# Context attentions of small heads: values of two periods and pieces of two periods in turn between the two blocks of a period

## The chip, the cores and the metric

The kernel runs on one core of a Trainium2 chip. The metric is the device time of one execution in microseconds (us); lower is better. Before the change three runs gave 2829.77 us as their median, from 2824.37 to 2834.39. The engines are called by the profile's names: PE (matmuls), PEld (loads of a matmul's stationary operand, which overlap PE), DVE (vector), ACT (activation), POOL and SP (which issues the transfers).

## The reference, cut to what matters

The reference is a decoder of four layers on 4 sequences of 256 tokens of width 128, in fp32. Two of its twelve blocks concern us: the cross attentions of layers 0 and 2, which attend to a context of 1601 rows of width 96 with 16 heads of 8.

```
q = (x @ Wq).reshape(B, N, 16, 8);  k, v likewise from the context (1601 rows)
scores = einsum('bhid,bhjd->bhij', q, k) * 8 ** -0.5      # layer 0 also masks
attn = softmax(scores, axis=-1)
out = einsum('bhij,bhjd->bhid', attn, v).reshape(B, N, 128)
```

Layer 0 multiplies the result by Wo, layer 2 sends it through a small feed forward net; each then adds the residual and normalises. The rest (band attention, two mixtures of experts, self attentions, linear attention, a wide cross attention, a quantised layer) is the same in both kernels.

## The kernel before, in words

The kernel is one program of eight stages. The stages `l0_xattn` (L1105) and `l2_xattn` (L1545) both call `context_heads` (L832), which the change rewrites in part. It works on 16 groups, each a batch element and four heads; a head sits in a strip of 32 partitions, so the matmuls of four heads can run on the PE at once, each in a strip of 32 rows of the array.

A group takes 7 periods, numbered p over the whole stage. The softmax needs the largest score of each query before it can take exponentials, so each group is worked through twice:

- `maxima` (L881) computes scores with the queries on the output's partitions, 458 keys at a time, and reduces them on DVE (L898) to a maximum. After the seventh part one more reduction (L904) writes the maxima to a padded tile.
- `shift` (L954) transposes the maxima on the PE and subtracts them (L535, DVE) from the queries.
- `scores` (L907), 9 periods after the maxima of the same group, computes shifted scores the other way round, for 256 keys, as two accumulations of 128 keys; ACT takes the exponential (L921) into tiles `E`.
- `sums` (L924), 10 periods after, multiplies the values with `E` and accumulates in one PSUM bank, `acc`, of which there is one (`bufs=1`, L928). In the `sums` matmuls all 128 rows of the array work, in strips of 32 columns. After the seventh period of a group ACT copies `acc` away (L939).

In one period the maxima are computed for heads 0 and 1, then for heads 2 and 3; the scores for heads 2 and 3 first and then for 0 and 1. So a half of `maxima` and a half of `scores`, written one after the other, fill the array's four row strips. Such a pair of halves is called a block here: two maxima tiles and two score tiles. A period has two blocks; the first is called A and the second B.

The other pieces are called from a table `other`, by period: `queries`, `keys` (four parts), `values` (four parts) and `shift`. With them go the steps of generators in `later`, one step a period (`advance`, L366): the end of a group (transposes, division), the output projection, the residual, the norm, and behind them other blocks of the network (`l0_ffn` and the queries of layer 1 in one stage, the end of `block1` with `l2_attn`, L1471, and `l2_gate`, L1587, in the other). Some of these steps use POOL, and one issues the transfer of the weights `p3_0` on SP.

PE, DVE and ACT take their instructions in the order in which the program writes them (`manual_schedule`). PSUM holds 7 banks that are given out in turn by `misc` (L349) and the one bank of `acc`. A block takes four of the seven, a piece one or two. So a tile's bank is that of the seventh tile before it, and its first matmul waits until that one has been read. `E` tiles turn over in the same way.

Of the kernel before, what the change touches and what calls it, by code (L numbers as in the profile page):

```python
# [21 lines left out]
B, T, D = 4, 256, 128  # L22
P = 128
# [6 lines left out]
NE, FM = 8, 408  # L30
# [272 lines left out]
class Net:  # L303
# [528 lines left out]
    def context_heads(self, query, wk, wv, done):  # L832
# [6 lines left out]
        nc = self.nc  # L839
        groups = [(b, kt, r) for b in range(B) for kt in range(2) for r in range(2)]  # L840
        n_groups, n_pairs = len(groups), len(groups) // 2
        scale = 8**-0.5
        vs = []
        for i in range(3):
            t = self.tile(f"V{i}", [P, NCH, 4, SW], bufs=1)
# [61 lines left out]
        def scores(i, k, jp):  # L907
            cs = range(2 * k, min(2 * k + 2, NCH))
            kp = min(P, S2 - 2 * k * P)
            w = len(cs) * T  # L910
            heads = [(j, self.misc()) for j in range(2 * jp, 2 * jp + 2)]
            for c in cs:
                for j, ps in heads:
                    r = slice(SW * j, SW * j + KR)
                    o = (c - 2 * k) * T
                    self.mm(
                        ps[:kp, o : o + T], ks[i // 2][r, c * P : c * P + kp], q2s[i][r, :]
                    )
            for j, ps in heads:
                e = self.tile("E", [P, 512], bufs=8)  # L920
                nc.scalar.activation(e[:kp, :w], ps[:kp, :w], AF.Exp, scale=scale)  # L921
                es[i, k, j] = e

# [34 lines left out]
        for t in range(n_pairs):  # L958
            for at, what in (
                (-4, (queries, t)), (-3, (keys, t, 0)), (-2, (keys, t, 1)), (-1, (keys, t, 2)),  # L960
                (1, (keys, t, 3)), (7, (shift, 2 * t)), (14, (shift, 2 * t + 1)),
            ):
                other.setdefault(14 * t + at, []).append(what)
        for b in range(B):
# [2 lines left out]

        engines = {nc.tensor.engine, nc.vector.engine, nc.scalar.engine}
        with self.tc.manual_schedule(engines=engines):
            for p in range(-4, 7 * n_groups + 10):  # L970
                (m, s, v) = (
                    divmod(p - lag, 7) if 0 <= p - lag < 7 * n_groups else None
                    for lag in (0, 9, 10)
                )
                if m:
                    maxima(*m, 0)
                if s:
                    scores(*s, 1)
                if v:
                    sums(*v)  # L980
                if m:
                    maxima(*m, 1)
                if s:
                    scores(*s, 0)
                for f, *args in other.pop(p, ()):
                    f(*args)
                self.advance(later)
            while later:
                self.advance(later)

# [480 lines left out]
    def l2_attn(self, b):  # L1471
        nc = self.nc
        x, xT = self.x[b], self.xT[b]
        ps = self.misc()
        for n in range(NB):
            self.mm(ps[:, n * D : (n + 1) * D], xT[:, n * P : (n + 1) * P], self.w("p2", "Wq"))
        pq = ps[:, : NB * D].rearrange("p (n d) -> p n d", n=NB)
        neg = self.tile("neg", [P, NB])
        nc.vector.tensor_reduce(neg, pq, AX.X, ALU.max, negate=True)
        q = self.tile("q", [P, NB, D], bufs=1)  # L1480
        sums = self.tile("sums", [P, NB])
        for n in range(NB):
            nc.scalar.activation(
                q[:, n, :], pq[:, n, :], AF.Exp, bias=neg[:, n : n + 1],
                accum_out=sums[:, n : n + 1],
            )
        ps = self.misc()
        self.mm(ps[:, :T], self.w("p2", "Wk"), xT)
        neg = self.tile("neg2", [P, 1])
        nc.vector.tensor_reduce(neg, ps[:, :T], AX.X, ALU.max, negate=True)  # L1490
        kT = self.tile("kT", [P, T], bufs=1)
        rk = self.tile("rec2", [P, 1])
        nc.scalar.activation(kT, ps[:, :T], AF.Exp, bias=neg, accum_out=rk)
        yield
        nc.vector.reciprocal(rk, rk)
        rec = self.tile("recs", [P, NB])
        nc.vector.reciprocal(rec, sums)
        for n in range(NB):
            nc.vector.tensor_scalar(
                q[:, n, :], q[:, n, :], rec[:, n : n + 1], D**-0.5, ALU.mult, ALU.mult  # L1500
            )
        ps = self.misc()
        for n in range(NB):
            nc.tensor.transpose(
                ps[:, n * P : (n + 1) * P], kT[:, n * P : (n + 1) * P], self.ident
            )
        for n in range(NB):
            self.mm(
                ps[:, T + n * D : T + (n + 1) * D], xT[:, n * P : (n + 1) * P],
                self.w("p2", "Wv"),  # L1510
            )
        kv = self.tile("kv", [P, 2, NB, D], bufs=1)
        nc.scalar.copy(kv.rearrange("p k n d -> p (k n d)"), ps)
        yield
        qT = self.transposed(q, "qT", engine=nc.scalar)
        yield
        ps = self.misc()
        for n in range(NB):
            self.mm(ps[:, :D], kv[:, 0, n, :], kv[:, 1, n, :], start=n == 0, stop=n == NB - 1)
        cx = self.tile("cx", [P, D], bufs=1)  # L1520
        nc.vector.tensor_scalar_mul(cx, ps[:, :D], rk)
        yield
        yield
        ps = self.misc()
        self.mm(ps[:, :T], cx, qT)
        aT = self.tile("aT", [P, T], bufs=1)
        nc.scalar.copy(aT, ps[:, :T])
        yield
        yield
        ps = self.misc()  # L1530
        for n in range(NB):
            to = ps[:, n * D : (n + 1) * D]
            self.mm(to, aT[:, n * P : (n + 1) * P], self.w("p2", "Wo"), stop=False)
            self.bias_mm(to, self.w("p2", "bo", 1))
        y = self.residual(b, ps[:, : NB * D])
        z = yield from self.normed_steps(y, "xn")
        wide = [P, NB, D]
        nc.gpsimd.tensor_mul(z, z, self.w("p2", "gamma").unsqueeze(1).broadcast_to(wide))
        nc.gpsimd.tensor_add(z, z, self.w("p2", "beta").unsqueeze(1).broadcast_to(wide))
        yield  # L1540
        y = self.y()
        nc.vector.tensor_add(y, z, x)
        yield from self.block_end_steps(b, y)
# [43 lines left out]
    def l2_gate(self, b):  # L1587

        nc = self.nc
        wide = [P, NB, NE]  # L1590
        ps = self.misc()
        for n in range(NB):
            to = ps[:, n * NE : (n + 1) * NE]
            self.mm(to, self.xT[b][:, n * P : (n + 1) * P], self.w("p2", "gw"), stop=False)
            self.bias_mm(to, self.w("p2", "gb", 1))
        pl = ps[:, : NB * NE].rearrange("p (n e) -> p n e", n=NB)
        neg = self.tile("neg", [P, NB])
        nc.vector.tensor_reduce(neg, pl, AX.X, ALU.max, negate=True)
        s = self.tile("gate", wide)
        sums = self.tile("sums", [P, NB])  # L1600
        for n in range(NB):
            nc.scalar.activation(
                s[:, n, :], pl[:, n, :], AF.Exp, bias=neg[:, n : n + 1],
                accum_out=sums[:, n : n + 1],
            )
        yield
        rec = self.tile("recs", [P, NB])
        nc.vector.reciprocal(rec, sums)
        nc.vector.tensor_mul(s, s, rec.unsqueeze(2).broadcast_to(wide))
        v1, one1 = self.top(s)  # L1610
        yield
        v2, one2 = self.top(self.without(s, one1))
        yield
        tot = self.tile("p", [P, NB])
        nc.vector.scalar_tensor_tensor(tot, v1, 1e-20, v2, ALU.add, ALU.add)
        nc.vector.reciprocal(tot, tot)
        nc.vector.tensor_mul(v1, v1, tot)
        nc.vector.tensor_mul(v2, v2, tot)
        nc.vector.tensor_mul(one1, one1, v1.unsqueeze(2).broadcast_to(wide))
        nc.vector.tensor_mul(one2, one2, v2.unsqueeze(2).broadcast_to(wide))  # L1620
        gate = self.tile("gates", wide, bufs=4, pool=self.act)
        nc.vector.tensor_add(gate, one1, one2)
        yield
        ps = self.misc()
        for n in range(NB):
            nc.tensor.transpose(ps[:NE, n * P : (n + 1) * P], gate[:, n, :], self.ident)
        wT = self.tile("wT", [NE, T])
        nc.scalar.copy(wT, ps[:NE, :T])
        yield
        ps = self.misc()  # L1630
        for n in range(NB):
            self.mm(
                ps[:, n * D : (n + 1) * D], wT[:, n * P : (n + 1) * P], self.w("p2", "db", NE)
            )
        return gate, self.residual(b, ps[:, : NB * D])
# [496 lines left out]
```

## Time and profile before

| what | value |
|---|---|
| median of 3 runs | 2829.77 us (2824.37 to 2834.39) |
| the profiled execution: its own time, its span | 2829.03 us, 2827.2 us |
| PE, DVE, ACT busy in the span | 95%, 64%, 54% |
| `l0_xattn`: first maxima to last `sums` matmul | 49.7 to 544.7 us |
| `l2_xattn`: the same | 841.9 to 1344.5 us |
| window 73 to 515 us (full periods of the first): PE, DVE, ACT busy | 433.75, 283.13, 246.41 of 442 us |
| window 875 to 1316 us (full periods of the second) | 432.86, 285.51, 237.48 of 441 us |

An instruction's line gives what it writes and reads (`one` is a tile from `misc`). `one<-K,Q` are the maxima, `one<-Q,K` the scores, `acc<-E,V` the sums, `one<-ctx,w` the keys, `one<-xT,w` the queries. An fp32 matmul shows as two passes, each with its own weight load, so `x16` of `acc<-E,V` is eight matmuls of the program. Matmuls in different strips overlap, and PE counts as busy as long as one of them is running.

### The profile page before, as it was taken

Reading aid. Unit: us, or ns where it says so; the run is one execution under the profiler, and the core shown is the slowest. Engines: PE = TensorE matmul, PEld = TensorE weight load, DVE = VectorE, ACT = ScalarE, POOL = GpSimd, SP = SyncE. Lnnn points to the kernel's source line nnn. Section 1 sums busy time; section 2 is a strip of 40 time slices with the busy share of each in tenths; the row PEclk is TensorE's granted clock in tenths of the full one; section 3 lists DMA queues with packets and bytes.
Section 4 is the critical chain, followed back from the end, with each engine's and each line's share of the span. In section 5 each row is a group of like instructions: output and inputs, shape, how many; then the busy total and the mean of one; then the engine's idle time right before and its main releaser. Section 6 shows DMA issues by size and latency. Waiting matters only on the chain.

```text
span 2827.2 us, 62963 instructions
## 1 busy us (share of the span) xinstructions
PE 2696.4 (95%) x27003; PEld 1776.1 (63%) x27003; DVE 1803.9 (64%) x3946; ACT 1533.0 (54%) x2943; POOL 178.4 (6%) x191
## 2 busy tenths in 40 slices
PE   7999999898889999999999999998999999999997
PEld 4555565566655555555897777776656666666664
DVE  6656666364567665664455766665757777777775
ACT  2555555455534555555553444445656666666564
POOL 2000110110010000000001111101100000000000
PEclk9999999999989999999999999999999999999999
DMA  3000000000020000000002000000000000000000
GB/s 114 1 2 1 2 1 2 1 1 1 1 79 23 1 2 1 1 2 1 1 1 103 2 14 2 2 2 2 2 1 2 3 2 2 3 1 2 3 1 3
DMA packets 5223, 27.65 MB, mean 10 GB/s; under 512 B 584, under 2 KB 2764, under 8 KB 3408
## 3 DMA queue, kind: packets, MB, share of 16 engines
q1 hardware_dynamic: 4944, 23.62, 2.4%
q8 instruction: 212, 3.47, 0.5%
q14 instruction: 67, 0.55, 0.1%
HBM read 23.07 MB, written 0.52 MB: 8 GB/s over the span
## 4 chain that ended last, share of the span: by engine, by line
PE 87%; DVE 8%; ACT 2%; issue 1%; DMA 0%; POOL 0%; POOLq 0%; ACTq 0%; DVEq 0%; SPq 0%
PE one L388 63%; PE big L388 13%; PE acc L388 8%; DVE M L898 1%; PE one L533 1%; PE one L824 1%; PE one L461 1%; DVE St L1974 1%; DVE mpad L686 1%; DVE Ms L681 1%; ACT w L1313 0%; ACT E L720 0%; PE one L1323 0%; DVE w L1940 0%; DVE ln_st L475 0%
## 5 line engine op out<-in xcount | busy, mean ns | idle before, releaser
L898 DVE TENSOR_REDUCE M<-one 128x1 f32<-128x458 f32 (+3 forms) x1024 | 528.7, 568 | 292.2 <-PE one L388 291.0
L921 ACT ACTIVATE E<-one 128x512 f32<-128x512 f32 (+1 forms) x896 | 457.8, 563 | 424.0 <-PE one L388 423.7
L388 PE MATMUL one<-Q,K 32*128 32x256 f32 (+1 forms) x3328 | 532.8, 403 | 1.5 <-DVE M L898 1.5
L388 PE MATMUL one<-K,Q 32*128 32x458 f32 (+3 forms) x2048 | 459.2, 541 | 1.6 <-DVE M L898 1.6
L388 PEld LDWEIGHTS one<-Q,K 32*128 32x128 f32 (+1 forms) x3328 | 311.1, 180 | 62.4 <-DVE M L898 35.6
L1930 ACT COPY St<-big 128x1024 f32<-128x1024 f32 (+1 forms) x224 | 204.3, 959 | 159.8 <-PE big L388 159.8
L388 PEld LDWEIGHTS one<-K,Q 32*128 32x128 f32 x2048 | 171.3, 185 | 142.9 <-issue 79.9
L1974 DVE TENSOR_TENSOR St<-St,Mb 128x1024 f32<-128x1024 f32 (+1 forms) x224 | 245.3, 1142 | 1.8 <-ACT Mb L1968 1.8
L388 PE MATMUL acc<-E,V 128*32 128x256 f32 (+1 forms) x3328 | 234.1, 388 | 7.1 <-ACT E L921 7.1
L720 ACT ACTIVATE E<-one 128x384 f32<-128x384 f32 (+1 forms) x352 | 154.3, 525 | 143.9 <-PE one L388 143.7
L1981 ACT ACTIVATE St<-St 128x1024 f32<-128x1024 f32 (+1 forms) x224 | 215.1, 1014 | 25.4 <-DVE St L1974 25.3
L388 PE MATMUL big<-Q,K 64*128 64x256 f32 (+1 forms) x1664 | 214.4, 393 | 0.0
L388 PE MATMUL one<-St,V 128*64 128x256 f32 (+1 forms) x1664 | 204.1, 382 | 0.4
L481 POOL TENSOR_TENSOR ln_r<-ln_ve,half 128x2 f32<-128x2 f32 x92 | 71.0, 771 | 2104.5 <-DVE ln_ve L479 2047.0
L1940 DVE TENSOR_TENSOR w<-w,St 128x1024 f32<-128x1024 f32 (+1 forms) x160 | 178.7, 1117 | 34.7 <-ACT St L1930 27.5
L388 PE MATMUL one<-xT,w 128*128 128x256 f32 (+1 forms) x664 | 169.7, 396 | 18.6 <-DVE Q L1116 8.3
L681 DVE TENSOR_REDUCE Ms<-one 128x3 f32<-128x384 f32 x256 | 130.4, 552 | 84.8 <-PE one L388 84.6
L388 PEld LDWEIGHTS big<-Q,K 64*128 64x128 f32 (+1 forms) x1664 | 147.7, 183 | 57.4 <-issue 40.2
L388 PEld LDWEIGHTS acc<-E,V 128*32 128x32 f32 (+1 forms) x3328 | 87.5, 109 | 125.6 <-issue 70.8
L388 PEld LDWEIGHTS one<-St,V 128*64 128x64 f32 (+1 forms) x1664 | 113.5, 137 | 62.7 <-issue 14.6
L388 PEld LDWEIGHTS big<-w,ctx 96*64 96x64 f32 x1664 | 97.1, 137 | 54.0 <-issue 53.9
L388 PEld LDWEIGHTS one<-xT,w 128*128 128x128 f32 (+1 forms) x664 | 96.5, 180 | 49.5 <-issue 15.6
(308 smaller groups left out, 3978.0 us busy)
## 6 DMA issues: line engine op xcount, KB each, us to landing
w<-in_p SPq DMA_DIRECT2D x4, 1483.0 KB, 10.3
ctx<-in_ctx SPq DMA_DIRECT2D x4, 600.4 KB, 13.5
w<-in_down SPq DMA_DIRECT2D x1, 2112.0 KB
w<-in_up SPq DMA_DIRECT2D x1, 1632.0 KB, 6.3
w<-in_gp SPq DMA_DIRECT2D x1, 1632.0 KB
w<-in_p SPq DMA_DIRECT2D x1, 1536.0 KB, 15.1
w<-in_p SPq DMA_DIRECT2D x1, 1413.0 KB, 12.2
w<-in_p SPq DMA_DIRECT2D x1, 1382.0 KB
```

What stands on the lines that cost most here:

```text
L388: self.nc.tensor.matmul(out, lhsT, rhs, start=start, stop=stop)
L461: self.nc.tensor.transpose(ps[:, n * P : (n + 1) * P], x[:, n, :], self.ident)
L481: nc.gpsimd.tensor_tensor(rstd, ve, self.half[:, :NB], ALU.pow)
L533: self.nc.tensor.transpose(ps[:rows, n * P : (n + 1) * P], m4[:, n, :rows], self.ident)
L681: nc.vector.reduce_max(out=m[:, j, :], in_=ps[:, : 3 * P].rearrange("p (s c) -> p s c", c=P), axis=AX.X,)
L720: nc.scalar.activation(es[t, j], ps[:, :w], AF.Exp, scale=scale)
L898: nc.vector.reduce_max(out=ms[i][:, n, j, part : part + 1], in_=ps[:, at : at + hi - lo], axis=AX.X)
L921: nc.scalar.activation(e[:kp, :w], ps[:kp, :w], AF.Exp, scale=scale)
L1930: nc.scalar.copy(st[:kp, :, :nc_, :], ps[:kp, :, :nc_, :])
L1940: nc.vector.tensor_max(to, to, sts[u, k][:kp, :, :nc_, :])
L1974: nc.vector.tensor_sub(e, e, top[u][:kp].unsqueeze(2).broadcast_to([kp, 2, nc_, T]))
L1981: nc.scalar.activation(e, e, AF.Exp, scale=HD**-0.5)
```

## The change

Between block A and block B of a period now stand, in turn, the `sums` of two periods (p odd) or the pieces of two periods (p even). The step of `later` moves with them, from the end of the period to the place between the blocks. Nothing stands any longer between block B of one period and block A of the next. The even one of two `sums` comes 11 periods after its maxima instead of 10, so a stage runs two periods longer and `E` gets 10 buffers instead of 8. `shift(2 * t)` is entered a period later (8 instead of 7).

To make room in SBUF, four tiles outside `context_heads` lose a buffer or share one: in `l2_attn` `qT` has one buffer, `aT` takes the place of `kT`, and the normed tile is a `z` of its own with one buffer instead of one of the two `xn`; in `l2_gate` `wT` has one.

```
-                e = self.tile("E", [P, 512], bufs=8)
+                e = self.tile("E", [P, 512], bufs=10)
...
-                (1, (keys, t, 3)), (7, (shift, 2 * t)), (14, (shift, 2 * t + 1)),
+                (1, (keys, t, 3)), (8, (shift, 2 * t)), (14, (shift, 2 * t + 1)),
...
-            for p in range(-4, 7 * n_groups + 10):
-                (m, s, v) = (
+            for p in range(-4, 7 * n_groups + 12):
+                m, s, *vs_ = (
                     divmod(p - lag, 7) if 0 <= p - lag < 7 * n_groups else None
-                    for lag in (0, 9, 10)
+                    for lag in (0, 9, 11, 10)
                 )
                 if m:
                     maxima(*m, 0)
                 if s:
                     scores(*s, 1)
-                if v:
-                    sums(*v)
+                if p % 2:
+                    for v in vs_:
+                        if v:
+                            sums(*v)
+                else:
+                    for f, *args in other.pop(p, []) + other.pop(p + 1, []):
+                        f(*args)
+                self.advance(later)
                 if m:
                     maxima(*m, 1)
                 if s:
                     scores(*s, 0)
-                for f, *args in other.pop(p, ()):
-                    f(*args)
-                self.advance(later)
...
-        qT = self.transposed(q, "qT", engine=nc.scalar)
+        qT = self.transposed(q, "qT", bufs=1, engine=nc.scalar)
...
-        aT = self.tile("aT", [P, T], bufs=1)
+        aT = self.tile("kT", [P, T], bufs=1)
...
-        z = yield from self.normed_steps(y, "xn")
+        z = yield from self.normed_steps(y, "z", bufs=1)
...
-        wT = self.tile("wT", [NE, T])
+        wT = self.tile("wT", [NE, T], bufs=1)
```

## The prediction

> **What bounds the kernel now.** I read the page first: busy shares, the granted clock, the chain, the costliest groups.
>
> ```profile
> PE 2696.4 (95%) x27003; PEld 1776.1 (63%) x27003; DVE 1803.9 (64%) x3946; ACT 1533.0 (54%) x2943; POOL 178.4 (6%) x191
> PEclk9999999999989999999999999999999999999999
> PE 87%; DVE 8%; ACT 2%; issue 1%; DMA 0%; POOL 0%; POOLq 0%; ACTq 0%; DVEq 0%; SPq 0%
> L898 DVE TENSOR_REDUCE M<-one 128x1 f32<-128x458 f32 (+3 forms) x1024 | 528.7, 568 | 292.2 <-PE one L388 291.0
> L921 ACT ACTIVATE E<-one 128x512 f32<-128x512 f32 (+1 forms) x896 | 457.8, 563 | 424.0 <-PE one L388 423.7
> ```
>
> PE is the bound, at a full clock, and DVE and ACT wait for it. But a busy PE need not be a full one, so I went on to the timeline. First a period and a half with a piece (keys) between B and the next A:
>
> ```profile
> 204.27 1.07 PE L388 MATMUL acc<-E,V 128*32 128x256 f32 x16
> 205.27 0.65 PE L388 MATMUL one<-K,Q 32*128 32x454 f32 x2
> ...
> 206.33 1.17 DVE L898 TENSOR_REDUCE M<-one 128x1 f32<-128x454 f32 x2 [0.93 <-PE one L388]
> ...
> 206.34 1.04 PE L388 MATMUL one<-ctx,w 98*128 98x458 f32 x2
> ...
> 207.31 0.65 PE L388 MATMUL one<-K,Q 32*128 32x458 f32 x2
> ...
> 208.61 1.07 PE L388 MATMUL acc<-E,V 128*32 128x256 f32 x16
> ```
>
> From start to start: sums 1.00 us, B 1.07, keys 0.97, A 1.30. Next, a period that had no piece, so that A follows B directly:
>
> ```profile
> 108.61 0.65 PE L388 MATMUL one<-K,Q 32*128 32x458 f32 x2
> ...
> 109.59 0.55 PE L388 MATMUL one<-K,Q 32*128 32x458 f32 x2
> ...
> 109.68 2.26 DVE L898 TENSOR_REDUCE M<-one 128x1 f32<-128x458 f32 x4 [1.73 <-PE one L388]
> ...
> 110.36 0.72 PEld L388 LDWEIGHTS one<-Q,K 32*128 32x128 f32 x6 [0.58 <-DVE M L898]
> 110.37 1.13 PE L388 MATMUL one<-Q,K 32*128 32x256 f32 x6
> 111.17 1.09 ACT L921 ACTIVATE E<-one 128x512 f32<-128x512 f32 x2 [0.29 <-PE one L388]
> 111.42 1.07 PE L388 MATMUL acc<-E,V 128*32 128x256 f32 x16
> ```
>
> B starts at 108.61, A's maxima at 109.59, but A's last score tile waits until 110.36 for DVE, and the sums start at 111.42: 2.81 us for two blocks. The reason is the ring of 7 banks. A block takes 4, so A's fourth tile is the seventh after B's first, whose reduction (0.635 us) starts only 1.07 us after B does; 1.07 + 0.635 + 0.055 to the release = 1.76 us, and the tile then needs 1.05 more. A piece in between takes a bank and gives DVE time. The waits view of 49 to 545 us names this wait:
>
> ```profile
> PEld one L388 <- DVE M L898: 31.9, 88, 0.7
> ```
>
> I cut the PE's matmuls in 73 to 515 and 875 to 1316 us into stretches of one kind. Directly adjacent B and A: 38 pairs, 108.0 us, mean 2.842, lowest 2.803, 31 of them under 2.82, and 3.05 to 3.06 in four, where small DVE instructions of a `later` step stood before B's first reduction. With pieces between: 164 pairs, whose blocks alone take 403.1 us, mean 2.458. A stretch of sums takes 1.001 us, one of keys 0.966.
>
> **The change part by part.** The sum is made against the profiled execution: 2829.03 us, span 2827.2, 0.7 us below the median of the runs.
>
> *Pairs.* The changed kernel's order of matmuls shows that no piece is left between B and A: every pair is direct. The relation of fourth tile to B's first holds in each, since exactly four tiles lie in each block. 164 pairs change from 2.458 to 2.842: 164 x 0.384 = +63.0 us. Bounds: all at 2.803 gives 202 x 2.803 - 511.1 = +55.1; all at 3.06 +107.0. I take the mean, as the wait has the same causes and DVE's extra work before it is of the same kind.
>
> *Sums of two periods.* Matmuls of sums start 0.2155 us apart in groups of four, so eight matmuls stream for 0.862 us and 0.139 of 1.001 goes with changing from strips of rows to strips of columns and back. 224 stretches become 112: 112 x 0.139 = -15.6 us. Upper bound of the gain 0.235 each (a block of 1.097 us streams 0.862), -26.3; lower 0.
>
> The Trainium skill, "TensorEngine Tiling (Array Packing)", section Key Properties, says that changing the tiling mode drains the PE. The trace agrees, with 0.139 us on a stretch of sums. If that were all that counted, two adjacent blocks would cost at most 2 x 1.076 and the sum below would be near -99 us. The same page's section PSUM Bottleneck speaks against the change: tiling speeds up the matmuls, not the reading of PSUM. The row decides: 2.81 us for the adjacent pair.
>
> *Pieces together.* By the order, stretches of pieces between the first and last sums fall from 171 to 120. Keys stream 2 x 458 columns at 0.842 ns (0.2155 / 256) = 0.771 of 0.966, so each stretch saved gives 0.195: 51 x 0.195 = -9.9 us (0 to -17 at 0.33). Even periods without pieces leave four blocks adjacent, 18 times; the third begins without a change of mode, some 0.1 us early: -1.8.
>
> *Queries* move from behind B to behind A. Their second matmul waits for DVE's copy of the first, which now stands behind reductions that ended earlier: the first matmul to the second took 1.79 us (191.83 to 193.62); behind a direct pair DVE is free 0.52 us after its end, so 0.65 + 0.53 + 0.06 = 1.24. 14 x 0.55 = -7.7 us (0 to -8).
>
> *The one `acc` bank.* Sums 6 of an even group and 0 of the next now stand back to back, and between them lies ACT's copy of `acc` (0.378 us), queued behind both exponentials of A. In the pair above these end 3.65 us after B's start. Sums 6 stream 0.43 us from 2.81, so the next would start at 3.27; the copy ends at 3.65 + 0.38 = 4.03, released at 4.09: 0.82 us, 16 times = +13.1 (0 to +16). Behind the waiting matmuls stands B; DVE and ACT have then nothing to do.
>
> *The other moved steps at nothing.* Key and value copies (0.55 and 0.375 us on ACT) now go before B's exponentials instead of after: ACT ends A's exponentials 0.84 us after the pair and B's scores come 1.08 us after the piece, so there is room for two. `shift` (0.41 us DVE) ends about 1 us after A, before B's first reduction (0.58 + 1.07); its queries are wanted by A of the next period. If that cover went, each of 32 shifts could cost 0.4 us, +13. The `later` steps keep one per period; their POOL instructions and SP's one load keep their order on those queues, and whoever waits for them does so a period later as before. What they put on DVE in front of B's reduction is in the mean of 2.842. `E` with 10 buffers: at most 10 are live, and the tile reused was summed just before. The two extra periods only finish loops; the last sums stay in period 121.
>
> *Buffers outside.* The four runs of `l2_attn` are at least 27 us apart (`kT` at 783.6, 810.7, 851.9, 928.5) and each is through with `aT` within 31 us, before the next begins its `kT`; `wT` is written every 60 us or more. Nothing; no row excludes a fraction of a us either way.
>
> Sum: 63.0 - 15.6 - 9.9 - 1.8 - 7.7 + 13.1 = +41.1. 2829.0 + 41.1 = 2870 us.
>
> **The rivals.** *Faster: the pair costs less.* If DVE freed the bank sooner, or PE went on with other rows meanwhile, the pair nears 2 x 1.076 = 2.152: 202 x 2.152 - 511.1 = -76.4, and with the rest -98: 2731 us. It decides below (511.1 + 21.9) / 202 = 2.64 us a pair. For it speak only the drains; against it all 38 direct pairs.
>
> *Much slower: DVE comes late.* If the pieces between A and B (queries' copies, shifts, norms, top-k) hold up B's first reduction regularly, the pair is 3.06 us: +107.0 - 21.9 = +85, 2914 us. For it: the four pairs near 3.06 after such work. Against it: most slots hold keys or sums, which put nothing on DVE.
>
> *A draw.* The pairs at 2.803, no `acc` wait and the greater gains: 55.1 - 26.3 - 17 - 1.8 - 8 = +2, 2831 us. It needs every term at its end.
>
> **How the numbers follow.** Forecast 0.70; late DVE 0.13; faster 0.10; draw 0.07. The forecast's own range is 2848 to 2893, from the wait on `acc` gone and 0.05 us less a pair to 0.1 us more a pair. The range must leave out no more than 0.2: 2838 to 2916 takes in the forecast and late DVE. Within 0.3% (8.5 us) is about what a measurement here can't tell from no change. Faster 0.10; same 0.06, most of the draw; slower 0.84.
>
> **What would show it.** In the changed profile: `one` L388 waiting for DVE `M` L898 some 200 times at up to 0.7 us in the two stages, instead of 175 of mixed kinds; B to the sums' start 2.8 us; sums of two periods in 1.86; sixteen waits of `acc` for ACT `acc_sb` L939 of 0.8 us; PE's instructions the same in number; the stages 20 us longer each, and nothing changed after 1345 us but a shift. The prediction is wrong if direct pairs take below 2.64 us, or if the pieces' PE instructions wait for what the moved `later` steps produce.

## The result and the profile after

| | before | after |
|---|---|---|
| median of 4 runs each, same chip | 2827.07 us (2824.22 to 2834.39) | 2868.86 us (2856.17 to 2869.46) |
| ratio, 95% interval | | 1.0133 [1.0098, 1.0168]: slower |
| the profiled execution: its time, its span | 2829.03, 2827.2 us | 2869.46, 2867.7 us |

The forecast was 2870 us, in a range of 2838 to 2916. The page of the changed kernel shows the same number of PE instructions and more time for them. Lines below the loop are numbered three higher than before.

```profile
PE 2720.4 (95%) x27003; PEld 1828.3 (64%) x27003; DVE 1799.0 (63%) x3946; ACT 1535.5 (54%) x2943; POOL 178.1 (6%) x191
PEclk7899999999999999999999999999999999999999
PE 85%; DVE 9%; ACT 3%; issue 2%; DMA 0%; POOL 0%; POOLq 0%; ACTq 0%; DVEq 0%; SPq 0%
L898 DVE TENSOR_REDUCE M<-one 128x1 f32<-128x458 f32 (+3 forms) x1024 | 515.2, 565 | 296.8 <-PE one L388 295.3
L921 ACT ACTIVATE E<-one 128x512 f32<-128x512 f32 (+1 forms) x896 | 452.2, 565 | 365.5 <-PE one L388 364.3
```

DVE and ACT do the same work in nearly the same time; PE is busy 24 us longer, and its loads 52 us longer. The first slices of the clock stand at 7 and 8 instead of 9; that is a matter of its own, below. The view of waits over the whole span (total us, times, longest) names the wait that the forecast counted on. Before, the first of these lines had 66.3 us in 174 waits.

```profile
PEld one L388 <- DVE M L898: 130.3, 251, 2.1
PEld acc L388 <- ACT acc_sb L939: 18.7, 16, 2.2
```

Asked for the two stages alone (97 to 580 and 910 to 1386 us), the same view gives 219 of the first waits, 116.6 us together, the longest 0.9 us in the first stage and 2.1 us in the second; the forecast had some 200 of at most 0.7 us.

The timeline of the changed kernel, a little over one period (start, duration, engine): a direct pair, two parts of keys, the next pair, the sums of two periods.

```profile
284.62 0.65 PE L388 MATMUL one<-K,Q 32*128 32x458 f32 x2
...
285.68 2.26 DVE L898 TENSOR_REDUCE M<-one 128x1 f32<-128x458 f32 x4 [1.85 <-PE one L388]
...
286.37 0.72 PEld L388 LDWEIGHTS one<-Q,K 32*128 32x128 f32 x6 [0.58 <-DVE M L898]
286.37 1.13 PE L388 MATMUL one<-Q,K 32*128 32x256 f32 x6
287.43 1.81 PE L388 MATMUL one<-ctx,w 98*128 98x458 f32 x4
...
289.17 0.65 PE L388 MATMUL one<-K,Q 32*128 32x458 f32 x2
...
290.92 0.72 PEld L388 LDWEIGHTS one<-Q,K 32*128 32x128 f32 x6 [0.58 <-DVE M L898]
...
291.98 0.42 PE L388 MATMUL acc<-E,V 128*32 128x256 f32 x4
```

Both pairs take 2.81 us (284.62 to 287.43, 289.17 to 291.98), and in both the last score tile waits for DVE's first reduction, as in the periods of the kernel before that had no piece. The two parts of keys between them take 1.74 us, where two separate ones took 1.93.

**Where the 40.5 us between the two profiled spans lie.** I cut PE's matmuls into stretches of one kind, in periods 12 to 110 of both stages, which both kernels work through in full:

| us, first and second stage together | before | after | difference | forecast |
|---|---|---|---|---|
| blocks | 495.2 | 550.8 | +55.6 | +61.2 |
| pieces | 167.5 in 173 stretches | 152.6 in 140 | -14.9 | -17.6 |
| sums | 185.0 in 196 stretches | 181.1 in 98 | -3.9 | -2.5 |
| sum | 847.6 | 884.5 | +36.9 | +41.1 |

The forecast column holds the terms of the prediction, which count more periods: 202 pairs instead of 196, and all 224 stretches of sums. A few small matmuls run inside a block and count as stretches of pieces of their own, 13 before and 27 after; without them 160 stretches became 113. Outside this cut lie +18.6 us up to period 12 of the first stage, -4.0 and -4.6 in the two tails (from period 110), -4.3 between the stages and -1.9 at the start of the second; after 1385 us nothing. Together +40.7. That the sum of the forecast landed on the profiled execution is in part luck: the start, which it had not foreseen, stood against the tails and the rest, which it had not foreseen either.

### The profile page after: what moved, and what is told of

Same layout as the page of the kernel before. It is cut to its first block, busy times and chain, and to the rows that moved or that the text cites. A ratio compares the mean times of both kernels' runs of the same rounds, so it can differ in the third digit from the quotient of the medians.

```text
span 2867.7 us, 62948 instructions
## 1 busy us (share of the span) xinstructions
PE 2720.4 (95%) x27003; PEld 1828.3 (64%) x27003; DVE 1799.0 (63%) x3946; ACT 1535.5 (54%) x2943; POOL 178.1 (6%) x191
## 4 chain that ended last, share of the span: by engine, by line
PE 85%; DVE 9%; ACT 3%; issue 2%; DMA 0%; POOL 0%; POOLq 0%; ACTq 0%; DVEq 0%; SPq 0%
PE one L388 62%; PE big L388 13%; PE acc L388 7%; DVE M L898 1%; PE one L533 1%; ACT E L921 1%; PE one L824 1%; PE one L461 1%; DVE St L1977 1%; DVE mpad L686 1%; DVE Ms L681 1%; DVE ln_st L475 1%; PE one L1326 1%; ACT w L1316 0%; ACT E L720 0%
## 5 line engine op out<-in xcount | busy, mean ns | idle before, releaser
L898 DVE TENSOR_REDUCE M<-one 128x1 f32<-128x458 f32 (+3 forms) x1024 | 515.2, 565 | 296.8 <-PE one L388 295.3
L388 PE MATMUL one<-Q,K 32*128 32x256 f32 (+1 forms) x3328 | 550.5, 405 | 12.3 <-DVE M L898 10.4
L388 PE MATMUL one<-K,Q 32*128 32x458 f32 (+3 forms) x2048 | 441.5, 535 | 0.2 <-DVE M L898 0.2
L388 PEld LDWEIGHTS one<-Q,K 32*128 32x128 f32 (+1 forms) x3328 | 332.8, 182 | 143.2 <-DVE M L898 109.2
L388 PEld LDWEIGHTS one<-K,Q 32*128 32x128 f32 x2048 | 196.4, 190 | 70.8 <-issue 42.9
L388 PE MATMUL acc<-E,V 128*32 128x256 f32 (+1 forms) x3328 | 209.4, 383 | 11.6 <-ACT acc_sb L939 11.0
L388 PEld LDWEIGHTS acc<-E,V 128*32 128x32 f32 (+1 forms) x3328 | 95.9, 109 | 109.2 <-issue 37.2
L388 PEld LDWEIGHTS one<-xT,w 128*128 128x128 f32 (+1 forms) x664 | 96.7, 181 | 45.0 <-issue 16.5
## 6 DMA issues: line engine op xcount, KB each, us to landing
w<-in_p SPq DMA_DIRECT2D x4, 1483.0 KB, 10.2
w<-in_p SPq DMA_DIRECT2D x1, 1536.0 KB, 16.5
```

The costliest lines, as they stand in the source:

```text
L388: self.nc.tensor.matmul(out, lhsT, rhs, start=start, stop=stop)
L898: nc.vector.reduce_max(out=ms[i][:, n, j, part : part + 1], in_=ps[:, at : at + hi - lo], axis=AX.X)
```

## The experiments

They are called runs 1 to 11, by the numbers of the headings. Every ratio is against runs of the kernel before on the same chip at the same time. "Full periods" are periods 12 to 110 of each stage, cut as above: 424.75 and 422.89 us before, 444.94 and 439.54 us after.

### 1. The changed kernel again

The start's +18.6 us was not in the forecast, so the first question was whether it belongs to the change. No edit.

> The changed kernel once more, unaltered, to see how firm the first 100 us are. In its first profile 18.6 of the 41 us more lay before period 12 of the first stage: 5.3 us before the first maxima, where a DVE instruction of the norm of x (L486) stood beside POOL's zeroing, and 13.3 us in periods 0 to 12, where the granted clock was 0.5 from 37 to 75 and from 82 to 95 us (before: only from 38 to 48 us). Theory (chance of a few us decides in which window of the clock gate the key matmuls fall): executions spread over two values some 13 us apart, as 2856.2 and 2869.0 did, and a profile with a start like that of the kernel before would have a span near 2854. Rival (the new order of the first periods lowers the clock): every execution and the profile show the slow start, and the time stays within 2 us of 2869.

Measured: median 2868.66 us (2856.4 to 2873.55, 6 runs) against 2831.3; ratio 1.0121 [1.0101, 1.0140]. The profiled execution, the fastest of the six, took 2856.4 us. Its full periods are the same to 0.1 us (445.03 and 439.61), but its start costs only 2.7 us more than before. Busy time by window (length, then busy PE, PEld, DVE, ACT and POOL, granted clock, DMA share, GB/s), first in the profile of the result:

```profile
0.00:55.80 55.80, 33.46 (x130) 21.94 (x130) 27.26 (x60) 15.18 (x38) 18.97 (x31) 0.83 0.48 145
55.80:97.30 41.50, 40.87 (x186) 24.89 (x187) 27.04 (x58) 7.96 (x19) 0.00 (x0) 0.61 0.00 1
```

and here:

```profile
0.00:55.80 55.80, 38.14 (x169) 25.45 (x169) 28.10 (x71) 16.17 (x41) 19.02 (x31) 0.91 0.50 145
55.80:97.30 41.50, 40.86 (x301) 25.47 (x302) 29.34 (x63) 15.58 (x33) 0.00 (x0) 0.92 0.01 1
```

The same kernel, the same busy share of PE in the second window, and 186 matmuls against 301, at a clock of 0.61 against 0.92. So the start varies from execution to execution, and the 20 and 17 us in the full periods of the two stages do not. The six executions lie at 2856.4, 2860.6, 2868.4 to 2868.9 and 2873.4 to 2873.6 us: neither the two values of the theory nor the one of the rival.

### 2. The start in the order of before

```
-                if p % 2:
+                if p < 9:
+                    pass
+                elif p % 2:
...
-                self.advance(later)
+                if p >= 9:
+                    self.advance(later)
...
+                if p < 9:
+                    for f, *args in other.pop(p, ()):
+                        f(*args)
+                    self.advance(later)
```

Against the changed kernel. Up to period 9 there are only maxima and pieces; here the pieces stand at the end of the period as before. If the new order made the clock drop, most of the start's loss should go.

> The changed kernel with its pieces and later steps at the end of each period, as before the change, in periods below 9, and the new order from period 9 on. If the new order of the first periods costs the clock there: periods 0 to 12 of the first stage take 33 us as before instead of 46, and the time falls by 13 to 18 us, to 2851 to 2856. If chance decides: no firm change, the same two values as in the run of the unaltered changed kernel. The full periods 12 to 110 cost the same as in the changed kernel in either case (445 and 440 us).

Measured: 2866.47 us (2862.34 to 2874.46), ratio 1.0122 [1.0105, 1.0140]; profiled start +8.6 us, full periods 445.03 and 440.87. No firm gain, and not the 2851 to 2856 us that the order of the first nine periods would have given if it set the loss.

### 3. Half a reduction

```
+                    read = (hi - lo) // 2 if j == 2 else hi - lo
                     nc.vector.reduce_max(
-                        out=..., in_=ps[:, at : at + hi - lo], axis=AX.X
+                        out=..., in_=ps[:, at : at + read], axis=AX.X
```

The first reduction of block B (head 2) reads half of its columns, so that the bank comes free about 0.3 us earlier; the other half is left out of the maximum. No PE instruction changes.

> The changed kernel, but the first head of block B (head 2) reduces only the first half of its score columns to a maximum; the other half is left out of that maximum, all else is computed. Theory (A's last tile waits for the bank that this reduction reads): the reduction falls from 0.63 to 0.39 us, each direct pair from 2.81 to 2.57, and 196 pairs in the full periods of both stages give 47 us: 2869 - 47 = 2822, about the time of the kernel before. Rival (the pair is long because of the PE itself, its drains and weight loads, or because of ACT): the pair stays 2.8 and the time within 5 us of 2869.

Measured: 2811.89 us (2811.3 to 2820.09) against 2831.3; ratio 0.9933 [0.9917, 0.9949], 57 us below run 1 by the medians and 44 us below it by the two profiled executions, whose starts differ by 1.2 us. Full periods 423.46 and 418.14, 42.9 us less than in the changed kernel; a direct pair has a median of 2.575 us instead of 2.813. In its timeline the pair from 265.08 to 267.65:

```profile
265.08 0.65 PE L388 MATMUL one<-K,Q 32*128 32x458 f32 x2
...
266.14 2.04 DVE L899 TENSOR_REDUCE M<-one 128x1 f32<-128x229 f32 x4 [2.26 <-PE one L388]
...
266.60 0.72 PEld L388 LDWEIGHTS one<-Q,K 32*128 32x128 f32 x6 [0.34 <-DVE M L899]
...
267.65 0.59 PEld L388 LDWEIGHTS acc<-E,V 128*32 128x32 f32 x16 [0.33 <-issue]
```

The wait falls from 0.58 to 0.34 us and the pair by the same 0.24. This shows that DVE's first reduction, not the row strips or the weight loads, sets the length of a pair. Some 0.24 us a pair on one of DVE's reductions is worth more, in the full periods, than the change costs there (42.9 us against 36.9).

### 4. The ring of banks, with one bank less

```
-  ... 7 if stage[3:] == "xattn" else 8 ...
+  ... 6 if stage[3:] == "xattn" else 8 ...
```

With six banks A's fourth tile needs the bank of B's second maxima tile, one reduction later.

> The changed kernel with a ring of 6 banks instead of 7 in the two context stages. Theory (A's fourth tile waits for the bank of the seventh tile before it): with 6 banks the fourth waits for B's second reduction and the third for the first, so a direct pair takes 1.07 + 2 x 0.63 + 0.06 + 1.05 = 3.44 us instead of 2.81: 196 pairs of the full periods give +123 us, near 2990, and B after sums stays at 1.08 or little more. Rival (the second block waits for DVE as such, whatever the bank): the pair stays 2.8 and the time within 20 us of 2869.

Measured, in one execution: 3013.27 us against 2830.3. Full periods 517.06 and 497.47, a direct pair 3.355 us (median).

```profile
PEld one L388 <- DVE M L898: 171.1, 397, 2.1
```

One reduction in the path costs 0.54 us a pair; half of one gave 0.24 back. Both say the same of the ring. The pair stays below the 3.44 us expected, and the full periods rise by 130 us, where 123 were expected; the time as a whole is 23 us above the 2990 expected, at a mean granted clock of 0.964, and only one execution was taken.

### 5. Buffers alone

```
-                e = self.tile("E", [P, 512], bufs=8)
+                e = self.tile("E", [P, 512], bufs=10)
...
-        qT = self.transposed(q, "qT", engine=nc.scalar)
+        qT = self.transposed(q, "qT", bufs=1, engine=nc.scalar)
...
-        aT = self.tile("aT", [P, T], bufs=1)
+        aT = self.tile("kT", [P, T], bufs=1)
...
-        z = yield from self.normed_steps(y, "xn")
+        z = yield from self.normed_steps(y, "z", bufs=1)
...
-        wT = self.tile("wT", [NE, T])
+        wT = self.tile("wT", [NE, T], bufs=1)
```

> The kernel before with only the buffers changed: E with 10, qT, z and wT with one, aT in the place of kT. Theory: nothing, within 0.3% of the kernel before. Rival (a shared buffer makes l2_attn or l2_gate wait, or E's two more buffers let ACT run ahead): 10 us slower, or some us faster.

Measured: 2834.22 us (2830.68 to 2844.64, 10 runs), ratio 1.0009 [0.9995, 1.0024]; full periods 424.75 and 422.89, equal to before. Nothing, as forecast.

### 6. Sums of two periods alone

```
+                if p % 2:
+                    for v in vs_:
+                        if v:
+                            sums(*v)
...
                 for f, *args in other.pop(p, ()):
                     f(*args)
                 self.advance(later)
```

The sums are paired as in the change, but the pieces stay at the end of their periods. In half of the periods A and B now stand next to each other.

> Of the two parts, only the sums of two periods together, between A and B of an odd period; pieces and later steps stay at the end of their own period. In even periods A and B are then adjacent. Theory (an adjacent pair costs 2.81 us, blocks with something between them 2.46): 98 pairs A and B of the full periods become direct, 98 x 0.36 = +35 us, the sums themselves -4 us as measured in the changed kernel, the tail -8: about 2829 + 23 = 2852. Rival (fewer changes of the tiling mode decide): 112 stretches of sums fewer give -16 us, the wait on acc +13, the tail -8: 2818 or so.

Measured: 2828.63 us (2825.65 to 2841.3, 10 runs) against 2832.73, ratio 0.9993 [0.9978, 1.0008]. Full periods 424.46 and 422.55: blocks +5.6, sums +0.4, pieces -6.6 against before. My theory wanted +23 and is wrong here. The rival's 2818 was nearer, though not by its own terms: the sums, which were to gain the most, did not get shorter. The timeline shows why, at a direct pair, a part of keys and the next block:

```profile
264.65 0.65 PE L388 MATMUL one<-K,Q 32*128 32x458 f32 x2
...
265.72 2.26 DVE L898 TENSOR_REDUCE M<-one 128x1 f32<-128x458 f32 x4 [0.35 <-PE one L388]
...
266.41 1.12 PE L388 MATMUL one<-Q,K 32*128 32x256 f32 x6
267.47 1.04 PE L388 MATMUL one<-ctx,w 98*128 98x458 f32 x2
268.43 0.65 PE L388 MATMUL one<-K,Q 32*128 32x454 f32 x2
...
269.51 1.93 PE L388 MATMUL acc<-E,V 128*32 128x256 f32 x32
```

The pair costs its 2.82 us, but the block after the piece takes 1.08, where such a block took 1.37 before (162 blocks `A` behind a piece and ahead of sums: mean 1.370; 78 such here: 1.100). In a direct pair the second block's maxima run while its last score tile still waits, so their reductions end soon after the pair (267.98, 0.51 us behind it), and the block behind the piece finds its banks free. The price of a direct pair has to be taken net of the relief that it gives the next block. In the full change every such block is itself the first of a direct pair and can make little of the relief.

### 7. Pieces of two periods alone

```
+                if vs_[1]:
+                    sums(*vs_[1])
...
+                if p % 2 == 0:
+                    for f, *args in other.pop(p, []) + other.pop(p + 1, []):
+                        f(*args)
                 self.advance(later)
```

> Of the two parts, only the pieces of two periods together, at the end of an even period; sums stay between A and B of every period, the later step at the end of each. B of an odd period and the next A are then adjacent wherever later has nothing. Theory (adjacent pair 2.81 against 2.46): some 98 - 38 = 60 more direct pairs, fewer by those that a later step parts, 40 to 60 x 0.38 = +15 to +23 us, pieces -10: 2829 + 5 to +13. Rival (drains decide): 2829 - 10 = 2819.

Measured: 2848.48 us (2843.58 to 2850.26), ratio 1.0055 [1.0036, 1.0075]. Full periods 429.16 and 430.10, +11.6 together: blocks +17.7 (75 direct pairs of 2.781 us instead of 36), pieces -6.7. This is what the theory expected there; the median lies 15.7 us above the kernel before, where 5 to 13 were expected. The sums alone come out even, the pieces alone lose 12 us in these periods, and both together 37, so the two halves do not add. The likely reason, argued from run 6 and not isolated further: with one half alone some blocks keep a gap on both sides and take up the relief; with both, no block does.

### 8. The opposite: sums cut in two

```
+                split = m and s and v and v[1] < 6 and p not in other
...
-                    sums(*v)
+                    sums(*v, 0 if split else None)
...
+                if split:
+                    sums(*v, 1)
```

If a gap between blocks is worth more than a change of tiling, it should pay to make gaps. In a period that has no piece, half of the sums (one of its two chunks of 128 keys) goes between A and B and the other half behind B. `sums` gets an argument for the half.

> The kernel before; where a period has no piece of its own, the sums are cut in two: the matmuls of its first 128 keys between A and B, those of the second 128 behind B, so that B and the next A are parted. Theory (the direct pair is what costs, and 0.57 us of other work covers most of its 0.7 us wait): such a period takes 3.5 instead of 3.8 us; 30 to 38 of them give 8 to 12 us: 2829 - 10 = 2819. Rival (each change of mode costs, the wait is hidden anyway): one stretch more of 0.14 us each, +5 us.

Measured: 2823.3 us (2806.67 to 2831.34, 12 runs) against 2832.73, ratio 0.9962 [0.9947, 0.9978]: faster than before. Full periods 419.90 and 414.01, -13.7 together: blocks -20.4, sums +6.7 for 56 more stretches (0.12 us each); 30 to 38 had been expected. The median gains 9.4 us, as expected (8 to 12).

### 9. Sums cut in two, and the tail's sums together

```
+                tail = p >= 7 * n_groups
...
+                if tail:
+                    if p % 2:
+                        sums(*w)
+                        sums(*v)
+                elif v:
                     sums(*v, 0 if split else None)
```

In the last periods of a stage there are no maxima left. There most stretches of sums of before stood waiting for the exponentials (1.482 us, against 1.00 in full periods), and sums of two periods meet that wait half as often. So this kernel takes the tail from the change, with its buffers, and the cut sums elsewhere.

> The kernel before with sums cut in two where a period has no piece (as in the run with split sums, -13.7 us in the full periods), and in the last periods, where no maxima are left, the sums of two periods together as in the changed kernel, with its buffers. Theory: both gains hold and add up: -13.7 and in the two tails -8 (there sums stood 0.48 us each for the exponentials, and half as many stand so): 22 us below the kernel before. Rival (the tail's gain belongs to the order of pieces and the tail is ACT's): no more than the split's own gain, some 10 us.

Measured: 2813.8 us (2808.36 to 2818.64, 6 runs) against 2830.3 (11 runs), ratio 0.9935 [0.9917, 0.9953]. Full periods 419.92 and 415.67, tails -3.8 and -4.3. The median gains 16.5 us where I had expected 22. It beats both kernels. Its timeline, in periods without a piece:

```profile
113.09 0.65 PE L388 MATMUL one<-K,Q 32*128 32x458 f32 x2
...
114.17 0.64 PE L388 MATMUL acc<-E,V 128*32 128x256 f32 x8
...
114.74 0.65 PE L388 MATMUL one<-K,Q 32*128 32x458 f32 x2
...
115.91 0.64 PE L388 MATMUL acc<-E,V 128*32 128x256 f32 x8
116.48 0.65 PE L388 MATMUL one<-K,Q 32*128 32x458 f32 x2
```

From start to start the two blocks take 1.08 and 1.17 us and the half sums 0.57 each: 3.39 us for what took 2.81 + 1.00 = 3.81.

### 10 and 11. A warm array at the start

```
+            if self.stage_n == 0:
+                ps = self.misc()
+                for _ in range(6):
+                    self.mm(ps, self.ident, self.w("c", "band"))
```

Six matmuls whose result nobody reads, ahead of the first context stage, in the kernel before and in the changed one. If the clock at the start explains the difference that the full periods do not, it should be smaller between these two.

> The kernel before with six matmuls of 128 x 512 put on the PE at the start of the first context stage, whose result nobody reads: they only keep the PE at work for more than one window of the clock gate, so that the first periods run at the full clock in every execution. They take 5 to 10 us themselves. Expected: periods 0 to 12 of the first stage as in the profile of the kernel before (33 us), the time 2830 + 5 to 10 with a smaller spread.

> The changed kernel with the same six matmuls. Theory (the change costs 28 us in what repeats: +37 in full periods, -8.5 in the tails; what the median shows beyond that, some 10 us, is the clock of the first periods, which falls differently by chance): 28 us, at most 32, above the warmed kernel before. Rival (the changed order costs some 10 us more somewhere else): 38 us above it, as without the six matmuls.

Measured: before with them 2838.39 us (2833.09 to 2840.97, 12 runs) against 2830.16, ratio 1.0027 [1.0016, 1.0038], with a start 10.0 us longer in its profile; the changed kernel with them 2872.63 (2864.7 to 2885.0, 6 runs), ratio 1.0149 [1.0124, 1.0174]. The two are 34.2 us apart, between what the two explanations wanted (28 to 32, and 38). In the profiled executions they are 26.4 apart and the starts 1.0. The matmuls did not do what they were for: the changed kernel still ran at half clock from 76.9 to 83.7 us. The window of 76 to 84 us of that run:

```profile
76.00:84.00 8.00, 8.00 (x43) 5.89 (x40) 6.48 (x15) 2.49 (x5) 0.00 (x0) 0.57 0.00 0
```

PE is never idle in it. So the test by experiment is inconclusive. What can be had is a comparison of executions by the mean granted clock that each lists. Kernel before: at 0.983, 2829.0 to 2831.3 us; at 0.978, thirteen executions from 2834.5 to 2839.1, mean 2837.2. Changed kernel: at 0.983, 2856.2 and 2856.4; at 0.978, 2873.4 and 2873.6. So the change costs some 26 us at the better clock and 36 at the worse one. But the six executions of the changed kernel at the clocks between (0.979 to 0.982) lie 31 to 37 us above the mean of the kernel before at the same clock, so the 26 rest on two executions. They agree with what repeats in the profiles: 36.9 - 8.6 in the tails - 6.2 between the stages and at the second start = 22, and 24.7 for run 1 (27.4 between the spans, less 2.7 at the start). What the rest of the 37 to 42 us between the medians is made of stays open: the one profile that holds such a rest has it in the start. Whether the new order makes such executions more frequent, or only dearer, stays open too.

## Why the prediction was right, point by point

**The bound and the pair.** The mechanism held: PE waits in every direct pair for the bank that DVE's first reduction of B frees. The clearly separated direct pairs of the changed kernel have medians of 2.813 us (82 with the sums behind, mean 2.836) and 2.814 (64 with pieces behind, mean 2.747); the term used 2.842. The second mean is lower because most pairs whose second block holds the short seventh part of a group's scores take 2.33 us. Runs 3 and 4 show the cause by moving the wait both ways.

That the mean held is partly luck. Counted from B of period 12 to A of period 110, the changed kernel has 196 pairs with a mean of 2.805 us. Of these, 138 take 2.63 to 2.93 (mean 2.823); 36 take 2.19 to 2.33, most of them those with a short seventh part, which comes to 19.1 us less than 2.842 each; and 22 take 3.07 to 4.42 (mean 3.495), 14.4 us more. In the 22, other DVE instructions, of a `later` step or a piece (top-k, gates, norms, copies), stand in front of a reduction or between two. The prediction had such pairs in its mean, at 3.06. In the pair from 1079.00 to 1082.98 us, seven of them (L1611 to L1152, each 0.15 to 0.17 us) occupy DVE from 1079.93 on, and B's reductions start at 1081.25, where 1.07 us after the start of B would be 1080.07. The wait is then 1.24 us instead of 0.58:

```profile
1081.25 1.16 DVE L898 TENSOR_REDUCE M<-one 128x1 f32<-128x454 f32 x2
1081.92 0.72 PEld L388 LDWEIGHTS one<-Q,K 32*128 32x128 f32 x6 [1.24 <-DVE M L898]
```

The term came out at +55.6 instead of +61.2: the short pairs and the late ones nearly cancel, and the six pairs outside the cut hold some 2 us of the term.

**Four blocks in a row.** Mis-sized: the clean cases, eight of them, take 5.112 us, where the term had 2 x 2.842 - 0.1 = 5.58. Eight times 0.47 is 3.8 us; six of the eight lie in the cut, among the 36 above. The prediction corrected them for a change of mode; it missed what run 6 shows, that the block behind a pair finds its banks free.

**Sums.** Two periods together take 1.865 us against 1.86 forecast, so the 0.139 us for a change to the other tiling and back was right. The wait on the one `acc` bank came as described: sums across two groups take 2.267 us where they wait and 1.435 where they do not, 0.83 us against 0.82, 16 times. The line of waits above shows those 16.

**Pieces and queries.** 14.9 us gained, 17.6 forecast; queries' first matmul to the second takes 1.34 us (209.09 to 210.43) instead of 1.24, from 1.79 before.

**At nothing.** Buffers and the moved `shift` and `later` steps: run 5 shows the buffers at nothing. The steps are not wholly at nothing: what they put on DVE in front of B's reduction is part of the 22 late pairs above, whose waits reach 2.1 us where the forecast had at most 0.7. That is read from the trace, not isolated by a run.

**What the prediction missed.** The tails: -8.6 us, for a stretch of sums that waited 0.48 us for exponentials in most of the last periods. The trace of before had it, in stretches that I had left out of my cut of full periods. The windows of the last 38 us of the first stage before, and the last 35 after:

```profile
506.25:544.73 38.48, 35.19 (x374) 18.59 (x368) 9.05 (x20) 25.05 (x53) 10.55 (x1) 1.00 0.00 1
```

```profile
545.04:579.56 34.52, 31.86 (x373) 19.60 (x367) 8.53 (x18) 24.36 (x53) 10.54 (x1) 1.00 0.00 1
```

The same number of matmuls at the same clock, 4.0 us less. The other miss is the start, where the two profiled executions of the changed kernel lose 3 and 19 us. Of the 19, 5.3 lie before the first maxima, where L486 on DVE took 5.79 us instead of 1.07, and 13.3 in periods 0 to 12, where the granted clock was at half for longer. The total was right within 2 us because these misses stood on opposite sides, which is luck; the executions near 2856 us lie 14 below it. The stages were to be 20 us longer each. From the first maxima to the last sums they are 29.6 and 10.2 us longer in this profile, 19 and 11 in that of run 1.

**The rivals.** "The pair costs less" needed 2.64 us a pair; no direct pair of full blocks in this kernel came near it, only those of run 3, whose reduction is halved. "DVE comes late" needed 3.06 as a mean; 2.805 excludes it, though 22 pairs of 196 are that late or later. The draw needed every term at its end. The pairs came near theirs (2.805 against 2.803), but the wait on `acc` came, and neither sums nor pieces gained what it asked.

The Trainium skill's page "TensorEngine Tiling (Array Packing)", section Key Properties, says that a change of tiling mode drains the array. The runs fit this, with 0.137 us for each stretch of sums saved (a change there and back), and 0.12 for each that run 8 adds. The change buys 98 of these at the price of waits of 0.6 to 0.7 us.

## What to carry to other kernels

When tiles turn over in a short ring of banks, ask of each tile which earlier tile's reader must be done, and how long after that tile's start its reader ends: work of another kind between two bursts is then no interruption but the time in which the reader catches up. Saving changes of tiling mode by putting like with like removes that time; here spreading the sums out, and paying more changes, was the faster way. And the price of one adjacent pair can't be multiplied up or halved without asking what the pair does for its neighbours: pairing the sums alone came out even, pairing the pieces alone cost 12 us in the full periods, and both together 37.

## What was not expected of the hardware

*A low clock under a busy array.* In the profile of the result PE is busy for 40.87 of 41.5 us and the granted clock is 0.61; within that window it stood at half up to 74.8 us and from 81.6 to 95.3. The kernel before was at half only from 37.7 to 47.9 us, the same changed kernel in run 1 37.8 to 48.0 and 68.5 to 75.3. These are the periods of maxima only, with 32-row matmuls. The Trainium skill, "TensorE: Matmul & The Clock Gate", Part 1, says that some 3.4 us of sustained activity release the throttle; that differs from the first 19 us of this window, in which PE shows as busy at half clock, though "busy" in the trace need not be what the gate counts. Drops of 3.4, 6.8, 10.2 and 13.7 us occurred (73.2, 76.9, 65.8 and 81.6 us into different runs), steps that agree with that page's window.

*Two small DVE instructions that took 5.8 us together.* The two normalisations at L486 (L487 in runs 10 and 11) just ahead of the first context stage took 5.79 us in the profile of the result and 1.07 us in that of before, beside the same memsets on POOL:

```profile
39.33 5.79 DVE L486 TENSOR_SCALAR x<-y,ln_mv,ln_r 128x128 f32<-128x128 f32 x2 [0.81 <-POOL ln_r L481]
```

Runs 1 and 7 show 1.06 and 1.07 us, the nine others 5.55 or 5.79. Run 1 is the changed kernel itself, and run 5 has the code of before at that place, so the change does not decide it. What does stays open.
